# A graph network on one core: the first layer's transposes one entry ahead of its products, in two tiles, and self-loop sums formed in place in PSUM

## The chip, the cores and the metric

The kernel runs on one core of one Trainium2 chip. The metric is device time in microseconds of one launch, the median of three runs. TensorE (PE) multiplies and transposes into PSUM, VectorE (DVE) and ScalarE (ACT) do the work on elements, GpSimd (POOL) issues the indirect transfers, and SyncE (SP) issues most of the direct ones.

## The reference

Four layers are applied to x, of 32 entries with 512 nodes of 256 features each (float32). The matrix adj (512 x 512) is the same for all entries; each pair of nodes is linked with probability 1/128, made symmetric, and every node is linked to itself. Layers 0 and 3 are of one kind, with weights of their own:

```python
def _L0_gnn_ref(h_t, A_a, A_m, W1, b1, W2, b2, Wa, ba, Wm, bm, beta1, beta2, beta3):
    d = h_t.shape[-1]
    pre_u = jnp.einsum('bud,dk->buk', h_t, W1[:d])
    pre_v = jnp.einsum('bvd,dk->bvk', h_t, W1[d:])
    hidden = jax.nn.relu(pre_u[:, :, None, :] + pre_v[:, None, :, :] + b1)
    S = jax.nn.sigmoid(jnp.einsum('buvk,ko->buvo', hidden, W2)[..., 0] + b2[0])
    a_t = jnp.einsum('buv,bud->bvd', S * A_a, h_t)
    m_t = jnp.einsum('uv,bud->bvd', A_m, h_t) * h_t
    return beta1 * h_t + beta2 * (a_t @ Wa + ba) + beta3 * (m_t @ Wm + bm)
```

Since S is only used where adj isn't zero, the kernel computes it for the linked pairs alone. Layer 1 is z + relu((adj z) W^T + b). Layer 2 is an attention over adj: features data W1^T, logits from one column of them, a leaky relu, adj added, a softmax over rows, and the products of its weights with the features, added to data.

## The kernel before

The 32 entries go in 8 groups, t = 0 to 7, of NB = 4. One group passes through these streams, each a Python generator that issues one piece at each step:

- `first` (L806 to L822) prepares layer 0. For each entry it loads x (tile `h0`, L811 on SP), transposes it by `turned` (L571 to L580), stores the transposed tile to DRAM for later use (xT, L819, on ACT's queue), and calls `pre`.
- `edges` gathers rows of the products for all linked pairs from a table in DRAM (L646, POOL), forms relu(u + v) and its product with W2 on DVE (L731, L739, L747) and ACT (L717), and puts the sigmoids into a dense matrix in DRAM (L639, POOL).
- `middle` takes the group's entries one after the other through layers 0 to 2 and starts layer 3 with `pre` on yT. It holds the large products: mhT (L46 adj,h, then DVE's L801), L891 and L898 of layer 0, L912 and L46 adjT,zW of layer 1, L934, L950, the softmax on DVE and ACT (L959 to L964), its transposes on PE (L1003) with copies on ACT (L1004), and L46 eT,feats. The next entry's products with Wa (L46, function `hWa`) are placed between the L1003.
- a second `edges` and then `last` (L1094) do layer 3: loads of h and hT by L1008 and L1013, L1061 and L1073 on PE, the results out by L1105 and, for a group's last entry, L1114. The last group uses `last_before` and `last_behind` in place of `last`.

`weave` (L454 to L502) merges the streams by due times. The pieces of `first` and `last` are fillers: a list of sizes (FIRST_US, LAST_US) tells how much PE time each is taken to need, and they are put in where a piece of `middle` says that it leaves room. So `first` of a group runs inside `middle` of the group one or two before it, entry by entry, at places that are set when the program is built. A scheduler may still move instructions within the limits of their data and buffers; each engine then runs its own list in order, and so does each DMA queue's issuer.

`turned` makes an entry's transposed tile hT: for each of the two halves of the features, four transposes of 128 x 128 on PE (L578) into one PSUM bank, and one copy by ACT (L579) into the tile. The tile comes from a ring with the tag "hT" in a pool with one buffer. Layer 3's transposed input hT3 (L1013) has the same tag, so both share that one buffer. The loaded tiles `h0` and `h3` share a ring with the tag "h" and two buffers.

`pre` computes pre_u and pre_v for one entry in four chunks of 128 nodes. A chunk has a PSUM bank of 512 columns, u in the first 256 and v in the others; the four matrix multiplies of a pair of chunks are L592 (first half of the features) and L594 (second half), each shown by the profile as two matmul records. Then, for each chunk: DVE adds the bias to u into `puv` (L596), ACT copies v beside it (L597), DVE adds v and u + b into the tile `both` in SBUF (L599), and multiplies its relu by W2 with a running sum (L600): that sum is the logit of the nodes' links to themselves. The store of `puv` (256 KB) to the table (L604, on SP) is issued one chunk later by `settle`. `puv` has three buffers and `both` one. All of these products, and the transposes, take banks from one PSUM ring of seven.

Of the kernel before, what the change touches and what calls it, by code (L numbers as in the profile page):

```python
# [8 lines left out]
F32 = mybir.dt.float32  # L9
# [3 lines left out]
ALU = mybir.AluOpType  # L13
# [3 lines left out]
P = 128  # L17
N = 512
D = 256
NC = N // P  # L20
DC = D // P
G = 32
NB = 4
# [25 lines left out]
class Model:  # L49
# [37 lines left out]
    def load(self, name, shape, view, pool=None):  # L87
        t = (pool or self.const).tile(shape, F32, name=f"w_{name}")
        self.nc.scalar.dma_start(t, view)
        return t  # L90
# [332 lines left out]
class Sparse:  # L423
# [147 lines left out]
    def turned(self, h, name, tag=None):  # L571

        nc = self.nc
        hT = self.act.tile([P, DC, N], F32, name=name, tag=tag or name)
        for c in range(DC):
            pt = self.psum()
            for r in range(NC):
                nc.tensor.transpose(pt[:, r * P : (r + 1) * P], h[:, r, c * P : (c + 1) * P], self.m.ident)  # L578
            nc.scalar.copy(hT[:, c, :], pt)  # L579
        return hT  # L580

    def pre(self, g, b, hT):

        nc, w = self.nc, g.w
        rows = g.table.rearrange("(c p k) (b d) -> p c k b d", p=P, k=2, b=NB)
        for c in range(NC):
            cs = slice(c * P, (c + 1) * P)
            if c % 2 == 0:
                two = [self.psum() for _ in range(2)]
                for k, pp in enumerate(two):  # L590
                    ks = slice((c + k) * P, (c + k + 1) * P)
                    nc.tensor.matmul(pp, hT[:, 0, ks], w["W1"][:, 0::DC, :], start=True, stop=False)  # L592
            pp = two[c % 2]
            nc.tensor.matmul(pp, hT[:, 1, cs], w["W1"][:, 1::DC, :], start=False, stop=True)  # L594
            puv = self.small.tile([P, 2, D], F32, name="puv", bufs=3)
            nc.vector.tensor_tensor(puv[:, 0, :], pp[:, 0:D], w["b1bc"], ALU.add)  # L596
            nc.scalar.copy(puv[:, 1, :], pp[:, D:])  # L597
            both = self.small.tile([P, D], F32, name="both", bufs=1)
            nc.vector.tensor_tensor(both, pp[:, D:], puv[:, 0, :], ALU.add)  # L599
            nc.vector.scalar_tensor_tensor(  # L600
                both, both, 0.0, w["W2bc"], ALU.max, ALU.mult, accum_out=g.self_s[:, c, b : b + 1]
            )
            self.settle()
            self.later = lambda c=c, puv=puv: nc.sync.dma_start(rows[:, c, :, b, :], puv)  # L604
            yield
# [200 lines left out]
    def first(self, g, i):  # L806


        def load(b):
            h = self.act.tile([P, NC, D], F32, name="h0", tag="h", bufs=2)  # L810
            self.nc.sync.dma_start(h, self.xr[i + b])  # L811
            return h

        h = load(0)
        for b in range(NB):
            ahead = load(b + 1) if b < NB - 1 else None
            hT = self.turned(h, "hT0", "hT")
            yield
            self.nc.scalar.dma_start(self.xT[i + b], hT)  # L819
            yield from self.pre(g, b, hT)  # L820
            h = ahead
        self.settle()  # L822

    def middle_before(self, g0, i):
# [51 lines left out]
    def middle_one(self, g0, g3, b, i, SA, keep, given):  # L876
# [51 lines left out]
        if more:  # L928
            keep[1] = turned()
            ahead = None if given else self.hWa(g0, keep[1], 0)  # L930
# [78 lines left out]
        return h  # L1009

    def x2T_of(self, i):
        hT = self.act.tile([P, DC, N], F32, name="hT3", tag="hT")
        self.nc.sync.dma_start(hT, self.x2T[i])  # L1013
        return hT

# [98 lines left out]
        nc.sync.dma_start(self.outr[i + NB - 1], done)  # L1114


FIRST_US = [0.9, 2.6, 0.9, 2.6, 0.9]
LAST_US = [1.7, 1.7, 3.4, 3.4, 3.7, 3.7, 1.7, 1.7]


# [41 lines left out]
def sparse_path(ctx, m, counts, xr, outr, B):  # L1162
# [10 lines left out]
    for t in range(last + 1):  # L1173
# [17 lines left out]
        if t == last:  # L1191
            end -= 0.2
            edges3 = edge_times(end + 0.003, end + 0.02, end + 0.45, end + 0.46, LEAD_AT_ENDS)
            behind = end + 0.29, end + 0.45
        streams += [
            (sp.first(g0, t * NB), first, FIRST_US),
            (sp.edges(g0, ("yT", "mhT0", "hWa0") if t == 0 else ()), edges0, ""),
            (sp.middle(g0, g3, t * NB), spread(middle_shares(t == 0), start, end), "main"),
# [251 lines left out]
```

## Time and profile before

| what | value |
|---|---|
| runs | 2982.0 us median of 3 (2972.71 to 2986.93) |
| profiled execution | 2998.45 us, its span 2996.8 us, mean granted TensorE clock 0.959 |
| busy share of the span: PE, DVE, ACT, POOL | 90%, 77%, 45%, 52% |
| DMA | 677.30 MB, mean 226 GB/s |
| L592 on hT, 256 records | 141.5 us, 681 ns each |
| L592 on yT, 256 records | 120.9 us, 595 ns each |
| L578, 256 records | 35.4 us, 283 ns each |
| L579, 64 copies | 35.7 us, 586 ns each |
| stores of puv | 256, of 256 KB each |

One execution is profiled. Busy time counts the instructions of an engine; for each wait the profile names the instruction that released it, as "row of the waiting engine <- engine, tile and line of the releaser". Shares over the whole span mix stages: the first 300 us build the lists of links, the table's first rows and the first group's sigmoids, the groups follow each other with some 345 us each, and the last 150 us hold the end of layer 3 of the last group.

### The profile page before, as it was taken

To read this page: it belongs to the slowest core of one execution; us is meant where nothing else is said; L and a number is where in the kernel's file an instruction comes from. 1 tells how busy PE (TensorE), PEld (TensorE's weight loads), DVE (VectorE), ACT (ScalarE), POOL (GpSimd) and SP (SyncE) were. 2 spreads that over 40 slices of the span, in tenths; PEclk is the share of its full clock that TensorE was granted. 3 is DMA by queue.
4 is the path that set the end of the run, shared out by engine and by line. 5 is a ranking of instruction groups with operands and counts; after the bars stand their busy time and mean duration, and the time that the engine had idled before them with its cause. 6 is when DMAs were issued, how large, how long until landed. Compare 5 with 4: busy or idle time off the path is not lost. (4 is left out here: it accounts for less than half of the span.)

```text
span 2996.8 us, 32453 instructions
## 1 busy us (share of the span) xinstructions
PE 2690.0 (90%) x8645; PEld 1613.9 (54%) x8646; DVE 2307.1 (77%) x6035; ACT 1336.8 (45%) x4101; POOL 1555.3 (52%) x1328
## 2 busy tenths in 40 slices
PE   6367787989998999989999899989999899988998
PEld 3134344545664566546664466646565466644666
DVE  6874786889588885988778885888858896783494
ACT  3553454445344443544344443445434453453262
POOL 2662463646445673556536464466735564361183
PEclk9678998999999999999999999999999999999999
DMA  8875657796678867787677866687677866663474
GB/s 268 286 225 169 213 174 221 233 300 203 217 217 269 268 211 227 230 262 254 209 222 247 275 207 230 216 268 253 211 228 236 303 227 197 208 211 102 148 244 150
DMA packets 302143, 677.30 MB, mean 226 GB/s; under 512 B 52608, under 2 KB 170880, under 8 KB 293760
## 3 DMA queue, kind: packets, MB, share of 16 engines
q0 software_dynamic: 122688, 414.40, 42.9%
q1 hardware_dynamic: 160304, 223.52, 23.0%
q10 hardware_dynamic: 18960, 37.24, 3.4%
q8 instruction: 70, 1.15, 0.2%
q14 instruction: 121, 0.99, 0.1%
HBM read 529.02 MB, written 146.01 MB: 225 GB/s over the span
## 5 line engine op out<-in xcount | busy, mean ns | idle before, releaser
L646 POOL DMA_INDIRECT rows<-table,iv x552 | 679.0, 1230 | 795.5 <-DMA table<-puv 262.7
L639 POOL DMA_INDIRECT cells<-s,cell x576 | 697.6, 1211 | 420.6 <-DVE s L675 243.2
L731 DVE TENSOR_TENSOR rows<-rows,mine 128x1024 f32<-128x1024 f32 x552 | 666.4, 1215 | 101.4 <-DMA rows<-table,iv 72.8
L717 ACT ACTIVATE rows<-rows 128x256 f32<-128x256 f32 x1088 | 439.6, 406 | 445.4 <-DVE rows L739 396.6
L46 PE MATMUL pst<-adj,h 128*128 128x512 f32 x1024 | 452.2, 592 | 0.0
L747 DVE SCALAR_TENSOR_TENSOR rows<-rows,L_gnn_W2bc 128x256 f32<-128x256 f32 x1120 | 414.0, 417 | 1.6
L739 DVE SCALAR_TENSOR_TENSOR rows<-rows,L_gnn_W2bc 128x1024 f32<-128x1024 f32 x272 | 329.4, 1213 | 0.4
L46 PEld LDWEIGHTS pst<-adj,h 128*128 128x128 f32 x1024 | 192.8, 190 | 219.9 <-issue 217.6
L46 PE MATMUL pst<-L_gnn_Wa,hT 128*128 128x256 f32 x1024 | 248.8, 393 | 62.9 <-DMA hT<-xT 57.8
L46 PEld LDWEIGHTS pst<-L_gnn_Wa,hT 128*128 128x128 f32 x1024 | 198.9, 199 | 103.0 <-issue 59.2
L46 PE MATMUL pst<-eT,feats 128*128 128x512 f32 x512 | 237.7, 619 | 10.9 <-ACT eT L1004 10.9
L46 PE MATMUL pst<-adjT,zW 128*128 128x512 f32 x512 | 228.2, 599 | 11.6 <-ACT zW L916 9.7
L596 DVE TENSOR_TENSOR puv<-pst,bc_L_gnn_b 128x256 f32<-128x256 f32 x256 | 104.9, 416 | 162.4 <-DMA table<-puv 89.2
L597 ACT COPY puv<-pst 128x256 f32<-128x256 f32 x256 | 93.2, 371 | 288.1 <-DVE puv L596 225.9
L1061 PE MATMUL pst<-hWa,SA 128*128 128x256 f32 x896 | 220.3, 400 | 0.0
L1061 PEld LDWEIGHTS pst<-hWa,SA 128*128 128x128 f32 x896 | 213.8, 328 | 3.7 <-issue 1.7
L717 ACT ACTIVATION_READ_ACCUMULATOR rows<-rows 128x1 f32 x1088 | 204.7, 188 | 0.0
L860 ACT COPY flat<-SA 128x512 f32<-128x512 f32 x128 | 136.7, 1128 | 136.6 <-issue 62.9
L891 PE MATMUL pst<-flat,hWa 128*128 128x512 f32 x448 | 196.8, 592 | 0.0
L592 PE MATMUL pst<-w_L_gnn_W,hT 128*128 128x512 f32 x256 | 141.5, 681 | 53.9 <-ACT hT L579 36.5
L46 PEld LDWEIGHTS pst<-eT,feats 128*128 128x128 f32 x512 | 99.9, 198 | 133.2 <-issue 113.3
L46 PEld LDWEIGHTS pst<-adjT,zW 128*128 128x128 f32 x512 | 96.5, 191 | 133.4 <-issue 114.0
(176 smaller groups left out, 3984.2 us busy)
## 6 DMA issues: line engine op xcount, KB each, us to landing
table<-puv SPq DMA_DIRECT2D x256, 256.0 KB
SA<-cells POOLq DMA_DIRECT2D x64, 1024.0 KB
h<-in_x_dram SPq DMA_DIRECT2D x64, 512.0 KB
mine<-table SPq DMA_DIRECT2D x64, 512.0 KB
hT<-xT SPq DMA_DIRECT2D x36, 512.0 KB
xT<-hT ACTq DMA_DIRECT2D x32, 512.0 KB
x2T<-yT SPq DMA_DIRECT2D x32, 512.0 KB
x2s<-x ACTq DMA_DIRECT2D x64, 256.0 KB
```

The source lines that it names most:

```text
L46: nc.tensor.matmul(out, lhsT, rhs, start=(n == 0), stop=(n == len(pairs) - 1))
L592: nc.tensor.matmul(pp, hT[:, 0, ks], w["W1"][:, 0::DC, :], start=True, stop=False)
L596: nc.vector.tensor_tensor(puv[:, 0, :], pp[:, 0:D], w["b1bc"], ALU.add)
L639: ins = self.nc.gpsimd.indirect_dma_start(out=g.cells[half], out_offset=bass.IndirectOffsetOnAxis(ap=at, axis=0), in_=s, in_offset=None)
L646: self.nc.gpsimd.indirect_dma_start(out=rows, out_offset=None, in_=g.table, in_offset=bass.IndirectOffsetOnAxis(ap=at, axis=0))
L717: self.behind(nc.scalar.activation(part, part, AF.Identity, accum_out=g.s[:, k, b : b + 1]))
L731: self.behind(nc.vector.tensor_tensor(rows, rows, other, ALU.add))
L739: nc.vector.scalar_tensor_tensor(by_entry, by_entry, 0.0, w2, ALU.max, ALU.mult)
L747: nc.vector.scalar_tensor_tensor(part, part, 0.0, w["W2bc"], ALU.max, ALU.mult, accum_out=at)
L860: self.nc.scalar.copy(flat[:, r, :], SA[r][:, :, b])
L891: nc.tensor.matmul(pz, hWa[:, r, cs], flat[:, r, :], start=(r == 0), stop=False)
L1061: self.nc.tensor.matmul(pz[:, k * D : (k + 1) * D], SA[r][:, cs, b], hWa[:, r, :], start=(r + k == 0), stop=(alone and k == 1 and r == NC ...
```

## The change

In five places, the transposes of `first` are issued one entry ahead of its products, and the sum of u and v is formed in the PSUM bank that holds v.

```diff
     def turned(self, h, name, tag=None):
 
         nc = self.nc
-        hT = self.act.tile([P, DC, N], F32, name=name, tag=tag or name)
+        hT = self.act.tile([P, DC, N], F32, name=name, tag=tag or name, bufs=2)
...
             nc.scalar.copy(puv[:, 1, :], pp[:, D:])
-            both = self.small.tile([P, D], F32, name="both", bufs=1)
-            nc.vector.tensor_tensor(both, pp[:, D:], puv[:, 0, :], ALU.add)
+            both = pp[:, D:]
+            nc.vector.tensor_tensor(both, both, puv[:, 0, :], ALU.add)
             nc.vector.scalar_tensor_tensor(
                 both, both, 0.0, w["W2bc"], ALU.max, ALU.mult, accum_out=g.self_s[:, c, b : b + 1]
             )
...
-        h = load(0)
+        hs = [load(0), load(1)]
+        ahead = self.turned(hs.pop(0), "hT0", "hT")
+        yield
         for b in range(NB):
-            ahead = load(b + 1) if b < NB - 1 else None
-            hT = self.turned(h, "hT0", "hT")
-            yield
+            hT = ahead
             self.nc.scalar.dma_start(self.xT[i + b], hT)
+            if b < NB - 1:
+                ahead = self.turned(hs.pop(0), "hT0", "hT")
+                if b < NB - 2:
+                    hs.append(load(b + 2))
+                yield
             yield from self.pre(g, b, hT)
-            h = ahead
         self.settle()
...
     def x2T_of(self, i):
-        hT = self.act.tile([P, DC, N], F32, name="hT3", tag="hT")
+        hT = self.act.tile([P, DC, N], F32, name="hT3", tag="hT", bufs=2)
         self.nc.sync.dma_start(hT, self.x2T[i])
         return hT
...
-FIRST_US = [0.9, 2.6, 0.9, 2.6, 0.9]
+FIRST_US = [0.9] + [0.9, 2.6, 0.9, 2.6, 0.9] * (NB - 1) + [2.6, 0.9, 2.6, 0.9]
```

The ring "hT" now has two buffers, for `turned` and for hT3 alike. `first` loads entries 0 and 1 and transposes entry 0 before anything else; then, for each entry, it stores the transposed tile, transposes the next entry, loads the one after that, and only then issues the entry's products. The list of sizes follows the new order of pieces; the number of pieces is the same. In `pre`, for both layers, L599 writes into the bank that it reads, and L600 reads and writes there; the SBUF tile `both` is gone.

## The prediction

> **What bounds the kernel now.** I read the page's totals first, then busy time by stretches, the table of TensorE's waits, and the timeline of one steady group (t = 4).
>
> ```profile
> span 2996.8 us, 32453 instructions
> ...
> PE 2690.0 (90%) x8645; PEld 1613.9 (54%) x8646; DVE 2307.1 (77%) x6035; ACT 1336.8 (45%) x4101; POOL 1555.3 (52%) x1328
> ```
>
> ```profile
> 100.00:200.00 100.00, 49.83 (x124) 26.68 (x124) 90.26 (x189) 59.13 (x251) 67.63 (x50) 0.73 0.73 236
> ...
> 1000.00:1500.00 500.00, 479.08 (x1583) 293.86 (x1582) 405.39 (x1083) 222.94 (x668) 278.65 (x234) 0.99 0.72 236
> ```
>
> In the stretches the columns are length, then PE, PEld, DVE, ACT and POOL busy, granted clock, DMA share, GB/s. From 1000 to 1500 PE works 479 of 500 us, and the next two stretches of 500 us read 475 and 474: there a wait of PE is time, and some 21 to 26 us in 500 are left to win. From 100 to 200 VectorE is busy 90% and PE half: there a wait of PE is hidden. The waits of PE that bear on the change (total us, times, longest):
>
> ```profile
> PE pst L1003 <- DVE ex L964: 51.7, 27, 10.8
> PE pst L592 <- ACT hT L579: 36.5, 11, 4.9
> PE pst L46 <- DVE both L599: 16.2, 1, 16.2
> ```
>
> The second row is the change's target: products that wait for the copy of their transposes. By place, 10.0 of it falls in the first 100 us and 2.5 in the next hundred; the other 24.0 are six waits, one in each of the groups t = 2 to 7 (4.53, 3.60, 3.60, 3.58, 4.88, 3.80). In the timeline (start, us, idle before in brackets) they look like this:
>
> ```profile
> 1217.27 1.04 PE L578 MATMUL pst<-ident,h 128*128 128x128 f32 x8
> 1218.14 1.89 PE L46 MATMUL pst<-L_gnn_Wa,hT 128*128 128x256 f32 x8
> 1219.87 0.60 PE L1003 MATMUL pst<-ident,ex 128*128 128x128 f32 x4
> 1220.31 1.88 PE L592 MATMUL pst<-w_L_gnn_W,hT 128*128 128x512 f32 x4
> ...
> 1261.25 1.04 PE L578 MATMUL pst<-ident,h 128*128 128x128 f32 x8
> 1265.89 2.51 PE L592 MATMUL pst<-w_L_gnn_W,hT 128*128 128x512 f32 x4 [3.60 <-ACT hT L579]
> 1268.19 1.91 PE L594 MATMUL pst<-w_L_gnn_W,hT 128*128 128x512 f32 x2
> 1269.89 3.99 PE L912 MATMUL pst<-WT,hT 128*128 128x256 f32 x16
> 1273.72 1.02 PE L594 MATMUL pst<-w_L_gnn_W,hT 128*128 128x512 f32 x2
> ...
> 1302.50 1.98 PE L592 MATMUL pst<-w_L_gnn_W,hT 128*128 128x512 f32 x4 [2.08 <-DVE both L600]
> ```
>
> Entry 0's transposes (1217) are covered by other products. Entry 1's (1261) stand bare in front of their own products: ScalarE, in order behind an L717, copies late, and PE idles 3.60 us. Then it also runs slow: L592, L594 and L912 take from 1265.89 to 1273.72, 7.83 us, where the same pieces undisturbed take 1.72 + 0.86 + 3.45 = 6.03 (from starts at 1274.57, 1276.29, and at 1616.35 and 1619.80); the granted clock from 1265 to 1275 is 0.83, before and after it 1.00. Over the six groups this excess is 3.07 + 1.80 + 1.80 + 1.75 + 2.19 + 1.64 = 12.2 us. Entry 3 stalls again at 1302.50; the six waits there, put down to L600, L962, L963 or issue, make 13.5 us.
>
> **The change, part by part.** No instruction is added or removed; the sum is made against the profiled 2998.45 us (span 2996.8), which is 0.55% over the median of 2982.0.
>
> 1. Transposes one entry ahead. In the instruction list of the changed kernel the products at 1265.89 now follow entry 2's transposes and read entry 1's tile, copied some 40 us before. Removed: 24.0 + 12.2 = 36 us. VectorE, next in line, can follow: it idles 5.9 us in that group from 1268.7 to 1281.6 for PE. If DMA cannot follow (below), half is given back: bounds 18 to 36; I take 36.
>
> 2. What those transposes now stand behind. Entry 1's eight L578 move to between 1219.87's L1003 and the second half of L46's Wa products, before entry 0's products. Their input must have landed, and SP loads it late:
>
> ```profile
> 1217.31 0.39 SPq L1114 DMA_DIRECT2D out_dram<-h  x1
> 1218.33 2.56 SPq L811 DMA_DIRECT2D h<-in_x_dram  x2
> ```
>
> This load starts as entry 0's transposes release their buffer (1218.31) and competes with the out store; in the changed list it has the same place behind L1114 and the same wait for PE. Its last landing record is 4.66 us after its issue; in t = 3, 5, 6, 7 it is 5.52, 5.32, 4.63 and 5.70. PE reaches the moved transposes at 1220.31, 1.98 us after the issue. So a new wait of 3.55, 2.68, 3.35, 2.65 and 3.73 us (t = 3 to 7, each from its own starts), 16.0 us; the sixth group at their mean of 3.2 makes 19 us. Queued behind it on PE: the rest of the Wa products, the last L1003, L46's eT,feats and entry 0's products; nothing else on PE covers it. Bounds: two other loads by L811 (917.76, 1608.46), with no store beside them, landed after 3.8 us, so 1.8 x 6 = 11; the one at 1187.89 took 5.84, so 3.9 x 6 = 23. I take 19, from the loads themselves.
>
> The slow clock can follow this wait as well. The rows: 1.80 us lost behind 3.60 us, nothing behind 2.08 us. Six waits between these: 0 to 6 x 1.8 = 11; two are near 3.6, so I take 3.
>
> [...]
>
> 3. Entry 3. Its transposes now stand before L934, so the bare wait goes: 13.5 us. But this stretch is limited elsewhere: the DMA share from 1295 to 1305 is 1.00, VectorE's L596 waits up to 3.40 us there for puv stores, and L964 behind them on VectorE is what L1003 then waits for (3.30 us at 1313.38). So most of it comes back in that first row of the waits. Bounds 0 to 13.5; I take 5.
>
> 4. Sums in PSUM. Prices of the operations: L599 already reads PSUM, L600 does not.
>
> ```profile
> L599 DVE TENSOR_TENSOR both<-pst,puv 128x256 f32<-128x256 f32 x256 | 107.3, 419 | 30.7 <-ACT puv L597 21.5 <-ACT flat L860 0.6 <-issue 0.4
> L600 DVE SCALAR_TENSOR_TENSOR both<-both,L_gnn_W2bc 128x256 f32<-128x256 f32 x256 | 107.3, 419 | 2.8
> ```
>
> The same 419 ns with input from PSUM and from SBUF, so I price L600 unchanged; no row shows VectorE writing PSUM. The farthest pair, L801 (512 elements, PSUM in) 679 ns and L923 (SBUF only) 684, bounds it at -5 to +5 ns in each of 512, under 3 us of VectorE, which has some 18% free in the steady groups.
>
> [...]
>
> What can cost is the bank: it was free after L599 and is now held until L600 ends, 0.4 to 1.5 us longer by the ends of the pairs in the stretch 1235 to 1256. Six products instead of five of these now fall into layer 3's pre stretch, because entry 0's slide one place later; a bank was free there about 0.8 us before its use (1242.4 against 1243.22). Bounds 0 to 2 us a group in six groups, 0 to 12; I take 2, nearest the row, which mostly still fits.
>
> 5. Setup and group 1. 12.5 us of the removed wait lie there, with VectorE and DMA in front; in the list ScalarE's first L597 falls behind its string of DMA issues (until 38.7 us), which may delay the first table by some 3 us. Bounds -5 to +3; I take 0.
>
> 6. Second hT tile for layer 3, loads earlier on SP; L811's third load moves up directly behind the first two and can hold SP for entry 0's transposes, but the stores behind it come from later products. PE's waits for hT from x2T are 5.1 us in all, in the last stretch, where POOL's gathers and puts run without a gap until 2954. Bounds 0 to -5; I take 0.
>
> Sum: -36 + 19 + 3 - 5 + 2 = -17 us: 2998.45 - 17 = 2981; times 2982.0 / 2998.45 = **2965 us**. Its own range, with steps 2 to 4 half way to their bounds together: 2955 to 2978.
>
> **Rivals.**
>
> (b) No wait for entry 1's load. If it finds a free buffer before entry 0's transposes, steps 2's 19 + 3 vanish: -36 - 5 + 2 = -39, 2943 us. For: the diff asks for both loads up front. Against: two "h" buffers are shared with layer 3, and the list keeps the load behind the out store.
>
> (c) Given back at DMA. Entries 1 to 3 push their twelve stores of 256 KB through the same stretch, at a DMA share of 0.88, 0.77 and 1.00 already; if PE comes 5 us earlier and half of the 36 returns as L1003 waiting for L964, the sum is about +1: 2983 us. For: the 3.30 at 1313. Against: VectorE's and DMA's slack up to 1285.
>
> (d) Slower: banks. If VectorE's backlog fills the seven banks, each longer hold passes to PE in bursts of four products: 4 x 0.4 = 1.6 us at the least where nothing else covers it. Half of that, 0.75 us, in 56 entries (t = 1 to 7, both layers) is 42 us: -17 + 42 = +25, 3007 us. For: the third row of the waits is exactly such a wait, and L596 is often late (89.2 us for puv stores). Against: in the steady groups no such row appears today. It decides from 17 / 56 = 0.3 us an entry upwards.
>
> (e) That the order doesn't change: the list excludes it.
>
> **How the numbers follow.** Forecast 0.42, (b) 0.16, (c) 0.20, (d) 0.22. 0.5%, 15 us, is about what a measurement here tells from no change: 2967 to 2997 is the same. Faster: 0.29 of the forecast's 0.42, all of (b), 0.02 of (c): 0.47. Same: 0.13 + 0.15 of (c) + 0.02 of (d) = 0.30. Slower: 0.03 + 0.20 = 0.23. The range 2938 to 3006 leaves out about a third of (b) and half of (d), 0.16.
>
> **What would show it.** PE's row L592 from ACT hT falls from 36.5 to under 14, and the stretch after L898 keeps clock 1.00. A new row, PE L578 from DMA h, stands at 16 to 24 us; if it is missing, (b). L1003 from ex grows by some 8 us; by 20 or more, (c). New PE rows from DVE at L600 over 17 us, (d). L599 or L600 over 430 ns, or a slower setup, would break steps 4 and 5.

## The result, and the profile after

The changed kernel is slower: 2995.1 us in the median of 20 runs (2981.45 to 3003.53) against 2977.88 us of the kernel before (20 runs, 2968.41 to 2986.93). The ratio is 1.0050, with a 95% interval of 1.0038 to 1.0063: some 15 us lost, where 17 us were forecast to be won.

The page of the changed kernel, its busy time:

```profile
span 2992.8 us, 32257 instructions
...
PE 2696.4 (90%) x8645; PEld 1631.4 (55%) x8646; DVE 2309.9 (77%) x6035; ACT 1338.8 (45%) x4101; POOL 1571.4 (53%) x1328
```

Set beside the page of before, nothing seems lost: its span was 2996.8 us. But that execution, at 2998.45 us, was longer than every one of the 20 timed runs of its kernel. A second trace of the same kernel (run e1 below) has a span of 2973.1 us, and the changed kernel is compared with both.

PE's waits in the changed kernel (total us, times, longest; L938 is L934 of the kernel before, L916 is L912, L1007 is L1003):

```profile
PE pst L1007 <- DVE ex L968: 54.2, 29, 11.1
...
PE pst L938 <- DVE yT L927: 29.5, 18, 3.9
...
PE pst L916 <- DVE hT L903: 16.2, 10, 2.7
PE pst L578 <- DMA h<-in_x_dram: 12.6, 5, 2.8
...
PE pst L592 <- ACT hT L579: 0.7, 1, 0.7
```

and in the second trace of the kernel before:

```profile
PE pst L1003 <- DVE ex L964: 47.8, 24, 11.2
PE pst L592 <- ACT hT L579: 44.4, 16, 4.6
...
PE pst L934 <- DVE yT L923: 9.3, 12, 2.7
PE pst L912 <- DVE hT L899: 8.6, 5, 3.6
```

The target is hit: 44.4 us of waiting for hT became 0.7. The new wait of L578 for its load is there, 12.6 us. But PE now waits 20 us more for yT, 8 more for L903's hT and 6 more for ex: 44 us less, 47 us more. All waits of PE together hardly moved: 290 us, 284 in the second trace of before, 300 in the first.

One such place in the timeline of PE, first in the changed kernel, then in the second trace of before, the same stretch of the same group:

```profile
1210.68 1.94 PE L578 MATMUL pst<-ident,h 128*128 128x128 f32 x8 [2.81 <-DMA h<-in_x_dram]
1212.41 2.71 PE L46 MATMUL pst<-L_gnn_Wa,hT 128*128 128x256 f32 x8
...
1272.11 1.04 PE L578 MATMUL pst<-ident,h 128*128 128x128 f32 x8
1274.58 2.00 PE L938 MATMUL pst<-WT,yT 128*128 128x257 f32 x8 [1.44 <-DVE s L675]
1279.77 3.79 PE L938 MATMUL pst<-WT,yT 128*128 128x257 f32 x8 [3.19 <-DVE yT L927]
1283.35 3.07 PE L592 MATMUL pst<-w_L_gnn_W,hT 128*128 128x512 f32 x4
```

```profile
1271.54 1.04 PE L578 MATMUL pst<-ident,h 128*128 128x128 f32 x8
1272.41 3.63 PE L934 MATMUL pst<-WT,yT 128*128 128x257 f32 x16
1275.88 1.88 PE L592 MATMUL pst<-w_L_gnn_W,hT 128*128 128x512 f32 x4
```

The sixteen L934 that ran in 3.63 us without a pause are torn by two waits in the changed kernel, and what follows runs at half the clock (the records have 0.5 from 1278.92 to 1285.75 us): 3.79 us for eight L938 where 2.00 is usual, 3.07 for four L592 where 1.88 is.

To see this over more than one place, I cut each trace at the first product of layer 1 (L912, or L916) of each entry, from entry 0 of t = 2 to entry 0 of t = 7: five groups of `middle`, in which `first` of t = 3 to 7 runs. "0 to 1" adds up the five stretches from entry 0's to entry 1's first such product, and so on. "Waits" is all idle time of PE in gaps of over 0.15 us (in e9 the profile names no releaser for 25.0 us of it); "half clock" is an estimate of the time lost to the clock, half of each record of the granted clock at 0.5. All in us:

| trace | 0 to 1 | 1 to 2 | 2 to 3 | 3 to 0 | sum | waits | half clock | rest |
|---|---|---|---|---|---|---|---|---|
| before, first trace | 431.0 | 442.4 | 414.4 | 439.5 | 1727.3 | 84.2 | 20.5 | 1622.6 |
| before, second trace (e1) | 428.8 | 428.3 | 409.8 | 439.1 | 1706.0 | 71.1 | 13.7 | 1621.2 |
| changed | 425.1 | 456.6 | 409.7 | 442.7 | 1734.1 | 83.1 | 32.4 | 1618.5 |
| sums in PSUM alone (e2) | 416.5 | 459.1 | 404.7 | 438.8 | 1719.2 | 77.6 | 18.8 | 1622.8 |
| order alone (e3) | 420.9 | 456.5 | 413.8 | 438.1 | 1729.3 | 84.5 | 23.9 | 1620.9 |
| order, half an entry ahead (e9) | 407.7 | 476.2 | 415.7 | 443.2 | 1742.8 | 93.3 | 30.7 | 1618.8 |

The rest is the same within 5 us: nearly every difference here is a wait or a slow clock. Against e1 the changed kernel loses 28 us in these groups, 12 of them in waits and 19 at half clock. The stretch from entry 0 to 1, where the bare transposes stood, became shorter in each variant; the one from 1 to 2 became longer by more. The two traces of one kernel differ by 21 us, so that single traces show where time sits, and the ratios of the timed runs decide.

The timed runs show the clock too: each lists its granted clock, and I estimate the time it cost as the span times one minus that clock. On average this is 130.2 us in the 20 runs of the changed kernel, and 118.0 us in the 124 runs of the kernel before that stand beside the experiments (115.3 to 120.3 by set). Of the 17 us between the average spans (2992.2 and 2975.0), some 12 are slow clock. Against the kernel before beside it, the order alone (e3) loses 20.3 us, 10.7 of them slow clock; the sums alone (e2) lose 8.5, 0.3 of them slow clock.

### The profile page after: what moved, and what is told of

It is laid out like the page before. It is cut to its first block, busy times and chain, and to the rows that moved or that the text cites. A ratio compares the mean times of both kernels' runs of the same rounds, so it can differ in the third digit from the quotient of the medians.

```text
span 2992.8 us, 32257 instructions
## 1 busy us (share of the span) xinstructions
PE 2696.4 (90%) x8645; PEld 1631.4 (55%) x8646; DVE 2309.9 (77%) x6035; ACT 1338.8 (45%) x4101; POOL 1571.4 (53%) x1328
## 5 line engine op out<-in xcount | busy, mean ns | idle before, releaser
L639 POOL DMA_INDIRECT cells<-s,cell x576 | 716.8, 1244 | 389.3 <-DVE s L675 217.3
L731 DVE TENSOR_TENSOR rows<-rows,mine 128x1024 f32<-128x1024 f32 x552 | 667.6, 1218 | 104.5 <-DMA rows<-table,iv 79.5
L46 PE MATMUL pst<-adj,h 128*128 128x512 f32 x1024 | 452.3, 592 | 0.3 <-DVE pst L600 0.3
L46 PEld LDWEIGHTS pst<-adj,h 128*128 128x128 f32 x1024 | 192.8, 190 | 220.3 <-issue 217.9
L46 PE MATMUL pst<-L_gnn_Wa,hT 128*128 128x256 f32 x1024 | 264.1, 411 | 50.3 <-DMA hT<-xT 50.3
L46 PEld LDWEIGHTS pst<-L_gnn_Wa,hT 128*128 128x128 f32 x1024 | 209.0, 209 | 89.9 <-ACT puv L597 26.5
L46 PE MATMUL pst<-eT,feats 128*128 128x512 f32 x512 | 230.4, 604 | 11.4 <-ACT eT L1008 11.4
L46 PE MATMUL pst<-adjT,zW 128*128 128x512 f32 x512 | 226.3, 595 | 4.7 <-ACT zW L920 4.5
L596 DVE TENSOR_TENSOR puv<-pst,bc_L_gnn_b 128x256 f32<-128x256 f32 x256 | 105.7, 417 | 132.0 <-DMA table<-puv 91.5
L46 PEld LDWEIGHTS pst<-eT,feats 128*128 128x128 f32 x512 | 97.9, 193 | 127.9 <-issue 112.1
L46 PEld LDWEIGHTS pst<-adjT,zW 128*128 128x128 f32 x512 | 96.1, 190 | 124.1 <-issue 115.3
L1007 PE MATMUL pst<-ident,ex 128*128 128x128 f32 x512 | 87.6, 309 | 82.7 <-DVE ex L968 54.2
```

What stands on the lines that cost most here:

```text
L46: nc.tensor.matmul(out, lhsT, rhs, start=(n == 0), stop=(n == len(pairs) - 1))
L639: ins = self.nc.gpsimd.indirect_dma_start(out=g.cells[half], out_offset=bass.IndirectOffsetOnAxis(ap=at, axis=0), in_=s, in_offset=None)
L731: self.behind(nc.vector.tensor_tensor(rows, rows, other, ALU.add))
```

## The experiments

Theories, as the expectations name them. A: from entry 1 on, the edges' chain of gathers and puts on POOL sets the pace through VectorE's fixed list, and the removed waits only covered for it; A1: the new wait for the load starts the loss; A2: the order itself does. B: the sums in PSUM cost by themselves. C: layer 3's earlier loads cost. D: the stores of puv set the pace there. P: PE does. All ratios are against the kernel before.

**e1, the kernel before again** (no edit).

> The kernel before, unchanged, for a second trace of it (the first one lasted 2998 us where its runs have a median of 2978). If the first trace is only slower in the setup, groups t = 3 to 7 show again waits of 3.6 to 4.9 us of L592 for ACT's hT, and each of these groups lasts 343 to 349 us. If the whole of it was slower, the groups are shorter by some 2 us each.

It took 2974.83 us, and its waits are those shown above. Each of the five groups is shorter (1706.0 against 1727.3 us in all), so the first trace was slow in them and not only in the setup: my sum was scaled from an execution with some 20 us of waits and slow clock too many.

**e2, the sums alone.**

```diff
-            both = self.small.tile([P, D], F32, name="both", bufs=1)
-            nc.vector.tensor_tensor(both, pp[:, D:], puv[:, 0, :], ALU.add)
+            both = pp[:, D:]
+            nc.vector.tensor_tensor(both, both, puv[:, 0, :], ALU.add)
```

> The kernel before with the one edit that the sums of L599 and L600 are formed in PSUM; one hT tile, the order of transposes as before. Theory A (the waits that were removed only covered for the chain of gathers and puts on POOL; the loss comes from the new order) expects 0.999 to 1.001. Theory B (sums in PSUM cost: in the changed kernel the read of L600's accumulator takes 142 ns against 80, and the bank is held longer) expects 1.003 to 1.006, the whole loss. In both the accumulator read takes 142 ns here.

1.0033 (1.0016 to 1.0049): B, as far as the time goes. The groups of instructions by shape, changed kernel, with the busy time and the mean after the bar:

```profile
L599 DVE TENSOR_TENSOR pst<-pst,puv 128x256 f32<-128x256 f32 x256 | 107.8, 429 | 38.8 <-ACT puv L597 34.1
L600 DVE SCALAR_TENSOR_TENSOR pst<-pst,L_gnn_W2bc 128x256 f32<-128x256 f32 x256 | 108.2, 431 | 1.9
L600 DVE DVE_READ_ACCUMULATOR pst<-pst,L_gnn_W2bc 128x1 f32 x256 | 36.2, 142 | 0.0
```

The sums themselves cost hardly more (429 and 431 ns against 419 each; busy 107.8 and 108.2 us against 107.3). The read of the accumulator behind L600 takes 142 ns here and 141 in e2, where it took 80: 256 x 62 ns = 16 us of VectorE.

**e3, the order alone** (the changed kernel with the sums back in SBUF).

```diff
-            both = pp[:, D:]
-            nc.vector.tensor_tensor(both, both, puv[:, 0, :], ALU.add)
+            both = self.small.tile([P, D], F32, name="both", bufs=1)
+            nc.vector.tensor_tensor(both, pp[:, D:], puv[:, 0, :], ALU.add)
...
+        w["b1bc"] = self.g0["b1bc"] if L == "L3_gnn" else self.bcast(f"{L}_b1", D)
```

> The changed kernel with the sums in SBUF again; to make room for that tile, layer 3 uses layer 0's b1 and its own b1 isn't loaded (1 KB per partition, one small load less in the setup). Theory A expects 1.003 to 1.006, the whole loss; theory B expects 0.994 to 1.000. The new wait of L578 for h, 2.3 to 2.8 us in each group, is there under both.

1.0068 (1.0045 to 1.0092). The order alone costs at least as much as the whole change; with the sums' 1.0033 it doesn't add up to 1.0050. B as the only cause is out.

**e4, the ring alone** (`bufs=2` at both places, nothing else; layer 3 with layer 0's b1).

> The kernel before with two hT tiles instead of one (for the transposes and for hT3 alike), the order of transposes and the sums as before; layer 3 uses layer 0's b1, whose own isn't loaded. Theories A and B expect 0.998 to 1.001. Theory C (layer 3's loads, issued earlier since they find a second tile, disturb the end of the groups and the tail, where the changed kernel's trace lost 4 us) expects 1.002 to 1.004.

0.9995 (0.9983 to 1.0007): C is out, and the shared b1 shows no effect in this build.

**e5, a third h buffer** for the changed kernel (the tile of layer 3, which shares the ring, has three too).

```diff
-            h = self.act.tile([P, NC, D], F32, name="h0", tag="h", bufs=2)
+            h = self.act.tile([P, NC, D], F32, name="h0", tag="h", bufs=3)
...
-        w["W1"] = self.load(f"{L}_W1", [P, 2 * DC, D], a[f"{L}_W1"].rearrange("(c p) k -> p c k", p=P))
+        if L == "L3_gnn":
+            w["W1"] = self.g0["W1"]
```

> The changed kernel with three h buffers instead of two, so that entry 1's load need not wait for entry 0's transposes; to make room, layer 3 uses layer 0's W1 and its own isn't loaded (one load of 512 KB less in the setup). Theory A1 (the wait of L578 for h starts the loss: it makes entry 0's products and yT late for VectorE, so the edges' L731 and then POOL's gathers are late) expects no row L578 from DMA h in the steady groups, and 0.997 to 1.001 against the kernel before. Theory A2 (the order itself costs, since one more product of pre stands ahead of the edges' L731 in VectorE's list) expects 1.003 to 1.005 and the same long stretch between the L916 of entries 1 and 2 (90 to 93 us against 85 to 86).

1.0019 (1.0004 to 1.0034), between the two expectations. Its companion, **e18**, is the changed kernel with nothing but the shared W1:

> The companion of the changed kernel with three h buffers (1.0019) and with five puv buffers (0.9966): the changed kernel with nothing else but layer 0's W1 in layer 3, whose own isn't loaded. If the shared W1 costs 0.36% here as in the pair with the sums alone (0.9959 against 0.9923), 1.007 to 1.010, and both edits are worth more than their ratios say. If it is neutral here, 1.003 to 1.007. If it is below 1.002, the three h buffers showed nothing.

1.0059 (1.0041 to 1.0078). So the third buffer is worth 1.0059 - 1.0019 = 0.4%, some 12 us. That this equals the 12.6 us of the wait that it removes is chance as far as the traces show: in the same five stretches PE now waits 11.1 us at L46 adj,h, and they take 424.9 us, where the changed kernel took 425.1 and e18 427.7. In the one at 1233 us PE starts just as VectorE ends a sum of `pre` (1233.2), which stood behind an L596 that waited 3.10 us for a store of puv; so I read this wait as one for a bank, held up by the stores. The difference of e5 and e18 sits from entry 1 to 2, 446.6 against 469.9 us.

**e6, extra work where the wait was**: in the changed kernel, four products in front of entry 1's.

```diff
+            if b == 1:
+                pp = self.psum()
+                for k in range(4):
+                    ks = slice(k * P, (k + 1) * P)
+                    self.nc.tensor.matmul(pp, hT[:, 0, ks], g.w["W1"][:, 0::DC, :], start=True, stop=True)
             yield from self.pre(g, b, hT)
```

> The changed kernel with four additional products of 128x512 (eight matmul records, some 3.4 us of PE) in front of entry 1's products of each group, where the removed wait was; nobody reads their results. If PE sets the pace there, 8 groups lose 3.4 us each: 1.005 + 0.009 = 1.014 against the kernel before (theory P). If the chain of gathers and puts sets it (theory A), the extra work is hidden by what PE waits for behind it, L938 for yT falls from some 3 us a group to under 1, and the ratio is 1.003 to 1.007.

1.0121 (1.0103 to 1.0139), 0.7% over the changed kernel, or 21 of the 27 us added. This speaks for P more than for A: PE's time there isn't simply free. From entry 1 to 2 the wait for yT did vanish (15.0 us in the changed kernel), as A expected, but the wait for ex took it over (21.2 us became 37.6). As I read it, time added in front of VectorE's fixed list delays what stands behind it in the list as well, edges included.

**e7 and e8, half the puts left out**, in the kernel before and in the changed one.

```diff
                 self.half = r[0]
-                self.put(g, *r)
+                self.odd = not self.odd
+                if self.odd or len(g.written[r[0]]) == 1:
+                    self.put(g, *r)
```

> The kernel before, with about every second put of sigmoids (L639) left out, so that those cells stay zero: 18 x 1.5 us less on POOL in each of the 16 streams. Its distance to the next kernel of this call is what counts. Theory A expects it itself clearly faster than the kernel before, 0.97 to 0.99, since POOL's chain is in front; theory P expects 0.99 to 1.00.

> The changed kernel, with the same puts left out. Theory A: with POOL relieved the removed waits come through, and it is 0.2 to 0.8% faster than the kernel before with half its puts. Theory A2 or B, in which the order of VectorE's work or the sums in PSUM cost by themselves: still 0.3 to 0.6% slower than that.

0.9959 (0.9944 to 0.9973) and 0.9896 (0.9881 to 0.9910). A had expected the first at 0.97 to 0.99, so POOL's chain alone doesn't set the pace of the kernel before; the second comes as A expected: with the puts halved, the changed kernel is 0.6% faster than the kernel before. In the five groups the two traces are even (1700.8 against 1700.6 us): the loss is gone there, and the rest of the gain lies before and after them. **e12**, the same puts left out with the sums in PSUM alone:

> The kernel before with the sums in PSUM and about every second put left out. If the sums cost through POOL's chain, the loss vanishes: 0.994 to 0.997 against the kernel before, as that with half the puts alone (0.9959). If they cost VectorE's or PE's time by themselves, 0.998 to 1.000.

0.9954 (0.9937 to 0.9971), equal to e7: the 0.33% of the sums is gone as well. With half the puts, neither part of the change costs anything. Leaving them out takes 322 us of busy time from POOL and 9216 small packets from the DMA queues at once (e1 and e7), so this doesn't tell which of the two matters.

**e9, the transposes half an entry ahead**, after two of the four chunks, and **e10**, the same with the sums in SBUF.

```diff
-            if b < NB - 1:
-                ahead = self.turned(hs.pop(0), "hT0", "hT")
...
-            yield from self.pre(g, b, hT)
+            for c, _ in enumerate(self.pre(g, b, hT)):
+                yield
+                if c == 1 and b < NB - 1:
+                    ahead = self.turned(hs.pop(0), "hT0", "hT")
+                    if b < NB - 2:
+                        hs.append(load(b + 2))
+                    yield
```

> The changed kernel with the transposes of the next entry not ahead of all of this entry's products but after the first two of its four chunks (two tiles and the sums in PSUM stay). Entry 1's transposes then come some 10 us later, when its load has landed, and only five products of pre stand in front of the edges' L731, as in the kernel before. If the wait for the load and the one more product are what the order costs, no row L578 from DMA h, and 0.997 to 1.002 against the kernel before; if any order with the transposes ahead costs, 1.003 to 1.006.

> The same with the sums in SBUF (layer 3 uses layer 0's b1, whose own isn't loaded). If the sums in PSUM cost by themselves, as the kernel with them alone showed (1.0033), this is 0.2 to 0.4% faster than the one before it in this call; if that cost was one of VectorE's order in that one build, they are within 0.15%, or it is the slower one, as without the sums in PSUM the full order was (1.0068 against 1.005).

1.0066 (1.0041 to 1.0090) and 1.0108 (1.0078 to 1.0137). This order has neither the old wait nor the new one (PE has no wait in the five stretches from entry 0 to 1), and these are 21 us shorter than in e1; the next five are 48 us longer. So the wait for the load and the sixth product are not needed for a loss of this size. What costs here is open in part: 21.8 us of waiting stand at L955 (the transposes of feats, L950 of the kernel before), for which the trace names no releaser. With this order the sums in PSUM seem to help.

**e11, the sums in PSUM in layer 0 only.**

> The kernel before with the sums in PSUM in layer 0's pre alone; layer 3's stay in SBUF. If the price is the instruction's (62 ns more at each read of the accumulator, the bank held longer), half of 0.33%: 1.001 to 1.0025. If it is the order of VectorE's list in the stretch of layer 3's pre, as the trace suggests (L801 and its wait for PE between two of the edges' L731), 0.999 to 1.001.

1.0010 (0.9994 to 1.0027): it holds both expectations and decides nothing.

**e13, e14, e15: more puv buffers**, four in the kernel before, five in it with the sums in PSUM, five in the changed kernel (with the shared W1).

```diff
-            puv = self.small.tile([P, 2, D], F32, name="puv", bufs=3)
+            puv = self.small.tile([P, 2, D], F32, name="puv", bufs=5)
```

> The kernel before with four puv buffers instead of three (room is there). VectorE's L596 waits 24 us for the stores of puv between the L912 of entries 1 and 2, in groups t = 3 to 7 together. Theory D (these stores set the pace there) expects that row under 12 us, and 0.994 to 0.998; theory A (POOL's gathers and puts do) expects 0.998 to 1.001, since VectorE then waits for the gathers instead.

> The kernel before with the sums in PSUM, which frees 1 KB, and five puv buffers. Theory D expects the 1.0033 of the sums alone to turn into 0.992 to 0.998; theory A expects 1.000 to 1.004.

> The changed kernel with five puv buffers instead of three; for the room layer 3 uses layer 0's W1 and its own isn't loaded. Between the L916 of entries 1 and 2 VectorE's L596 waits 36 us for the stores in the changed kernel. Theory D expects this to vanish, PE's waits for yT and ex behind it to shrink, and 0.992 to 0.999 against the kernel before. Theory A expects 1.002 to 1.006, with the waits of VectorE for the gathers grown by what those for the stores lose.

0.9964 (0.9949 to 0.9978), 0.9923 (0.9904 to 0.9941), 0.9966 (0.9951 to 0.9980). Against its companion e18 the last is 0.9% faster. VectorE's waits over the whole run, in the changed kernel and then in e15 (L735 and L600 are its L731 and L596):

```profile
DVE puv L596 <- DMA table<-puv: 91.5, 35, 5.4
DVE rows L731 <- DMA rows<-table,iv: 79.5, 61, 12.9
```

```profile
DVE rows L735 <- DMA rows<-table,iv: 120.6, 60, 13.0
```

Between entries 1 and 2 in the five groups, VectorE waited 36.2 us for stores and 15.2 for gathers in the changed kernel; in e15 1.6 and 47.5. D's ranges for the time hold in all three and A's in none; A is right about what is next: once the stores are out of the way, VectorE waits for the gathers. But the waits for stores there are no steady number, 24.2 us in e1 and 35.1 in the first trace of the same kernel. The row for the stores in e13 isn't under 12 us as D expected but 18.6, from 24.1.

**e16 and e17, with five puv buffers and the shared W1**: the order of e9, and the kernel before with the sums alone.

> Five puv buffers with the transposes of the next entry after two of this entry's chunks (sums in PSUM, two hT tiles; layer 3 uses layer 0's W1). The waits in front of entry 1's products are gone without a new wait for the load. If the stores were all that took the gain back, 0.986 to 0.991 against the kernel before and faster than the next kernel. If the order costs by itself (VectorE's list, gathers, slow clock behind a longer wait for yT), 0.994 to 0.999 and slower than the next kernel.

> The companion for it: the kernel before with the sums in PSUM and five puv buffers, and layer 0's W1 in layer 3 as in the other two with five buffers. 0.990 to 0.994 against the kernel before, as without the shared W1 (0.9923); if the shared W1 alone makes a difference of over 0.2%, the two kernels with the order ahead and five buffers must be compared with this one only.

0.9968 (0.9952 to 0.9985) and 0.9959 (0.9939 to 0.9979): no difference, and none to e15's 0.9966. The stores were then not all that took the gain back, since that expected 0.986 to 0.991 for e16. Whether the order still costs with five buffers depends on the companion: against e17 e15 is at 1.0007, against e14, which loads layer 3's own W1, at 1.0043; with three buffers the changed kernel is at 1.0017 against e2. All that five buffers surely bring is a faster kernel, with any order. e17 should have equalled e14's 0.9923; it is 0.36% above, with a single load less. I put such a difference down to the new build, in which VectorE's list may be set anew; what in it costs was not found. It is nearly as large as the 0.5% that the change loses, so a part of that loss can be of this kind.

## Why the prediction was wrong

**Step 1** failed, at "VectorE, next in line, can follow: it idles 5.9 us in that group", and with it the term of 36 us (24.0 of waits and 12.2 of slow clock behind them) and its lower bound of 18. The removal itself came as told (44.4 to 0.7 us), but the same time came back: 47 us more in other rows, and the slow clock, which steps 1 and 2 together let shrink by 9 us, grew by some 12 in the timed runs. VectorE's idle time was not slack that it could use (2.04 of the 5.9 us had no releaser in the profile, so not all of it is known to be for PE): its list is in order, and the items of `pre`, which wait for stores (L596, 91.5 us in the changed kernel), and those of the edges, which wait for gathers (L731, 79.5 us), stand in it between the ones that PE needs. In the changed kernel, just ahead of the second L927 that PE waits for (VectorE's timeline):

```profile
1274.43 1.22 DVE L731 TENSOR_TENSOR rows<-rows,mine 128x1024 f32<-128x1024 f32 x1
1277.19 1.23 DVE L731 TENSOR_TENSOR rows<-rows,mine 128x1024 f32<-128x1024 f32 x1 [1.55 <-DMA rows<-table,iv]
...
1279.02 0.69 DVE L927 TENSOR_TENSOR yT<-yT,hT 128x512 f32<-128x512 f32 x1
```

L927 needs nothing from the gather; it stands behind an L731 that does. Its own input from ScalarE (L926, 1275.16 to 1275.83) was there, and VectorE idled until 1277.19 all the same. And the gathers are late because POOL was held before, by VectorE: with the waits of L578, PE's products come late to it, and six products of `pre` instead of five stand in front of the edges' pair of L731. That pair starts at 1239.29 us in the changed kernel and at 1235.00 in e1, which is 3.8 us later once the offset of the two traces there (0.5 us) is taken off, and POOL with it (changed, then e1):

```profile
1230.20 0.99 POOL L646 DMA_INDIRECT rows<-table,iv  x1 [0.30 <-DVE pst L599]
1240.78 1.70 POOL L646 DMA_INDIRECT mine<-table,iu  x1 [9.59 <-DVE rows L731]
```

```profile
1230.20 1.00 POOL L639 DMA_INDIRECT cells<-s,cell  x1 [0.30 <-issue]
1236.49 1.69 POOL L646 DMA_INDIRECT mine<-table,iu  x1 [5.29 <-DVE rows L731]
```

From 1248 to 1289 us POOL then runs in the changed kernel with nothing but its 0.3 us between two transfers. That the stores and the puts matter to the loss is what e7, e8, e12 and e13 to e15 speak for. That this one delay of L731 starts it is read from the trace, not shown, and e9, which avoids it and loses as much, speaks against its being needed.

**Step 2** had the wait right, in place and cause: 12.6 us in five waits of up to 2.8, against 19 forecast for six: the loads landed some 4.5 us after their issue (2.5 us of waiting on average behind 2.1 us of work) where the first trace had 5.2 on average. The slow clock was mis-sized: 3 us forecast for this step, while the loss at half clock over the five groups went from 13.7 us (e1; 20.5 in the first trace) to 32.4. The premise "nothing behind 2.08 us" holds for the wait at 1302.50, but of the four such waits in the first trace two, at 956.24 and 1648.75, were followed by 3.41 us at half clock.

The records of the granted clock show how: in the changed kernel's trace, from entry 0 of t = 2 to 2990 us, it falls to 0.5 for 3.41, 6.83 or 10.24 us at a time. Behind the 2.81 us of L578 it was 3.41 us; behind the pair of 1.44 and 3.19 us of L938 it was 6.83, so 3.4 us lost for 4.6 us of waiting. The window in this stretch of the changed kernel (length, PE, PEld, DVE, ACT, POOL busy, clock, DMA share, GB/s), and in e1:

```profile
1277.00:1287.00 10.00, 7.23 (x14) 4.38 (x15) 9.01 (x25) 3.15 (x13) 8.17 (x7) 0.66 0.95 326
```

```profile
1277.00:1287.00 10.00, 8.22 (x29) 4.12 (x28) 8.71 (x31) 6.45 (x17) 7.87 (x8) 1.00 1.04 387
```

How long a wait it takes, these traces do not settle. In the changed kernel a wait of 1.97 us (L916, at 2043.33), with no other of over 0.15 us in the 8 us before, was enough, while one of 2.30 us (L578, at 864.19) was not followed by any slow clock. Of the 18 waits of 1.97 us or more in the five groups, 16 had a record at half clock begin between 1.4 us before their end and 1.5 us after it; of the five of L578 alone, those of 2.81, 2.61 and 2.44 us. So waits well below the two of some 3.6 us, on which the prediction's 3 us rested, were not free.

**Step 3** named the right resource, the stores of puv at a DMA share of 1.00, and drew too little from it: it let 8.5 of 13.5 us come back there, and the 36 of step 1 pass the same place untouched. Rival (c) had this mechanism, with half of the 36 returned; all of it returned and more, and at L938 and L916 rather than at L1003, whose wait for ex grew by 6.4 us against e1 and by 2.5 against the first trace.

**Step 4**: the sums were rightly priced as instructions, but the read of the accumulator was left out: 142 ns against 80, so 62 ns each and 16 us of VectorE. PE's waits for L600 and L599 didn't grow in the changed kernel (9.8 us for L600, against 16.4 for L599 in e1, nearly all in the setup), so the banks of rival (d) were not what cost there: the "slower" that it expected came by another way. Alone, the sums cost 0.33%, and nothing with half the puts.

**Steps 5 and 6**: entry 0 of t = 2 comes 6 us earlier than in e1 (825.7 against 831.5), and the end from entry 0 of t = 7 is 2.6 us shorter (433.0 against 435.6). Both are within what two traces of one kernel differ by.

**The base of the sum** was an execution 20 us above its median. Scaling by 2982.0 / 2998.45 spread this over all stages, while the second trace shows that 20 us of it sat in waits and slow clock of the five groups, the very places that steps 1 to 3 priced.

What stays open: what keeps VectorE late from entry 1 to 2, and so how much of the loss is the order's and how much that of one build; why the sums in PSUM cost 0.33% alone but seem to bring 0.2 to 0.4% with either order (e3 against the changed kernel, e10 against e9; the intervals overlap in both pairs), and why a shared W1 moved one build by 0.36% and another (e18 against the changed kernel, 1.0059 and 1.0050) hardly.

The version to keep is e14, the kernel before with the sums in PSUM and five puv buffers: 2949.77 us in the median of 6 runs beside 2972.39, 0.9923 (0.9904 to 0.9941). It uses the freed 1 KB for the buffers that VectorE waits for, and leaves the transposes where they were.

## What to carry to other kernels

A wait taken from the busiest engine is only won if what that engine needs next is ready sooner too (here 44 us less in one row came back as 47 in others); look at what stands in front of the next handover in the list of the engine that feeds it, and what that waits for, not at the engine's share of idle time. Where a wait is moved, price the clock with it: here 16 of 18 waits of 1.97 us or more went with 3.41 or 6.83 us at half clock, by estimate 1.7 or 3.4 us lost, and slow clock made up some 12 of the 17 us that the change lost. Take a second profile of the kernel before when its profiled run lies outside its timed runs.

## What the runs showed of the hardware

The read of the accumulator behind L600 took 142 ns with L600 in PSUM (changed kernel; 141 in e2) and 80 with L600 on SBUF (kernel before). L599 writing its result into PSUM took 429 ns (changed kernel) against 419 into SBUF (kernel before). In the changed kernel, from entry 0 of t = 2 to 2990 us, the granted clock fell to half for 3.41, 6.83 or 10.24 us at a time; it did so behind a single wait as short as 1.97 us (at 2043.33), though not behind one of 2.30 us (at 864.19), nor behind one of 2.08 us in the first trace of the kernel before (at 1302.50).
